# Row fetches split four and four behind the powers on GpSimd, in the last loop of a four-layer gated model

## The chip, the core and the metric

The kernel runs on one core of one Trainium2 chip. A core has five engines that run side by side, each through its own instructions in order: TensorE (PE, with its weight loads shown apart as PEld), VectorE (DVE), ScalarE (ACT), GpSimd (POOL) and SyncE (SP, which here only issues transfers). They wait for each other through semaphores. The metric is the device time of one execution, in microseconds, as the median of the runs.

## The reference

The input x has 32 sequences of 128 tokens with 128 features. Four layers follow each other, each an attention-like step and a feed-forward step whose results are added to x with a gate tanh(g). The last steps are the ones that matter here:

```python
x = x + jnp.tanh(g_ffn[2]) * _L2_ffn_ref(...)          # top 2 of 8 experts per token
x = x + jnp.tanh(g_xattn[3]) * _L3_xattn_ref(_layernorm(x), ctx_2048, ...)
x = x + jnp.tanh(g_ffn[3]) * _L3_ffn_ref(_layernorm(x), w_gate, w_up, w_down)
```

`_L2_ffn_ref` routes each token to two experts. `_L3_xattn_ref` (the depooling) takes a root-mean-square norm of its input, multiplies by a 128 x 128 matrix and a bias, and adds a decayed running sum of context patches. `_L3_ffn_ref` rounds its activations to integers by the largest value of each token, multiplies by ternary weights for gate and up, forms silu(gate) * up, rounds again in the same way and multiplies by the ternary down matrix.

## The kernel before, in words

The 32 sequences are handled as eight groups of four, so a group's x is a tile of 128 partitions (tokens) by 4 x 128 values. The x of all groups stays in SBUF for the whole kernel. The earlier layers and the mixture of experts run first. The experts leave their results in a table in DRAM, two rows for each token, and the running sums of the depooling lie in DRAM too. The last loop, which is all that the change touches, brings these together and runs the last feed-forward.

For each group g the loop has these parts:

- `fetch(g)` allocates the tiles `got` and `dp` (three buffers each), has SP load dp, and puts eight row fetches into the list `to_fetch`. A fetch is an indirect transfer issued by GpSimd (L821): it reads one row of the experts' table for each of 128 tokens. Eight of them fill `got`: four sequences by two experts. `move(to_fetch, n)` issues the first n of the list, or all.
- `depooled(g)` adds the fetched rows to x (eight instructions on VectorE, L833), takes the norm of x, transposes the result (TensorE, L272), scales it on ScalarE (hxT, L1344), multiplies it with `w_in` on top of dp (px, L1346 and L1348) and adds px to x (L280).
- `first(g)` takes the norm of x, quantizes it to integers (am, qt_x on VectorE, q_x on ScalarE), transposes it, forms the gate and up products (pg, pu, L1370 and L1372), silu on ScalarE (L1374) and the product h on VectorE (L1375).
- `second(g, h)` quantizes h (am, qt_h, q_h), transposes it, multiplies by the down matrix (po, L1391), scales it (L1396), adds it to x (L280) and has SP store x.

Both norms need a power of -0.5, and this power is computed on GpSimd. The statistics come from VectorE (L218 and L220). The norm of `depooled` computes two powers at once on eight columns (L254, tile w, operand made by L251 and L252). The norm of `first` computes one on four columns (L208, tile r, operand made by L207). VectorE then applies them (L241, tiles h and y). So the powers and the fetches share GpSimd, and GpSimd runs them in the order in which they stand.

The order within each engine is settled when the kernel is built: a scheduler sorts the instructions of an engine by what they depend on. The fetches are kept in program order. In the kernel before, `depooled(g)` calls `fetch(g + 1)` and `fetch(g + 2)` after its norm, and each `fetch` that has not been made yet issues its eight transfers at once. On GpSimd, eight fetches stand at the start, then the w of group 0, then sixteen fetches (groups 1 and 2), the w of group 1, eight fetches (group 3), the r of group 0, the w of group 2, eight fetches (group 4), the r of group 1, the w of group 3, and so on. The w of groups 6 and 7 have no fetches behind them.

Of the kernel before, what the change touches and what calls it, by code (L numbers as in the profile page):

```python
# [72 lines left out]
def tile_flamingo_gated(  # L73
# [22 lines left out]
    NG = B // NB  # L96
# [16 lines left out]
    xs = []  # L113
# [90 lines left out]
    def rsqrt(pool, v, eps=EPS):  # L204

        r = pool.tile([P, NB], F32, tag="r", name="r", bufs=4)
        nc.vector.tensor_scalar(r, v, eps, None, ALU.add)  # L207
        nc.gpsimd.tensor_tensor(r, r, m05.to_broadcast([P, NB]), ALU.pow)  # L208
        return r
# [30 lines left out]
                of = of.rearrange("p (h e d) -> p e h d", e=2, d=8)  # L240
            nc.vector.tensor_scalar(to, of, mv[:, b, 0:1], r[:, b : b + 1], ALU.subtract, ALU.mult)  # L241

    def layernorm(pool, a, tag="y", bufs=None, halves=False, again=None):

        mv = moments(pool, a)
        if again:

            w = pool.tile([P, 2, NB], F32, tag="w2", name="w2")  # L250
            nc.vector.tensor_scalar(w[:, 0], mv[:, :, 1], EPS, None, ALU.add)  # L251
            nc.vector.tensor_scalar(w[:, 1], mv[:, :, 1], 1.0 + EPS, EPS * EPS, ALU.mult, ALU.add)  # L252
            w2 = w.rearrange("p i b -> p (i b)")
            nc.gpsimd.tensor_tensor(w2, w2, m05.to_broadcast([P, 2 * NB]), ALU.pow)  # L254
            r, r2 = w[:, 0], w[:, 1]
        else:
            r = rsqrt(pool, mv[:, :, 1])
        y = None
        if tag:
            y = pool.tile([P, NB, D], F32, tag=tag, name="y", bufs=bufs)  # L260
            scaled(y, a, mv, r, halves)
        if not again:
            return y
        h = pool.tile([P, NB, D], F32, tag=again, name="h")
        scaled(h, a, mv, r2)
        return y, h
# [8 lines left out]
    def flat(a):  # L275
        return a.rearrange("p b s -> p (b s)")
# [114 lines left out]
    to_place, to_finish, to_fetch, to_store = [], [], [], []  # L391

    def move(queue, n=None):
        for do in queue[:n]:
            do()
        del queue[:n]
# [212 lines left out]
    class Routes:  # L609
# [205 lines left out]
        def fetch(self, pool, g, bufs=2):  # L815

            g -= self.begin
            got = pool.tile([P, 2, NB, D], F32, tag="got", name="got", bufs=bufs)

            def one(b, k):  # L820
                ins = nc.gpsimd.indirect_dma_start(  # L821
                    out=got[:, k, b, :], out_offset=None, in_=self.rows(),
                    in_offset=bass.IndirectOffsetOnAxis(ap=self.slot[:, g, k, b : b + 1], axis=0),
                )
                tc.keep_in_program_order(ins)

            to_fetch.extend(lambda b=b, k=k: one(b, k) for b in range(NB) for k in range(2))
            return got
# [77 lines left out]
    with ExitStack() as stack:  # L906
        w0 = load_weights(stack, W0, w0_d, W0.at, "w0")
        banks = attention_pools(stack, "s1", 1, 6)
        pool = banks[0]
# [210 lines left out]
    with ExitStack() as outer:  # L1120
# [3 lines left out]
        with ExitStack() as stack:  # L1124
            pool, psum = mlp_pools(stack, "f1")
# [24 lines left out]
        with ExitStack() as stack:  # L1150
            pool, psum_a, avs, _ = attention_pools(stack, "a2", 1, 4)
# [132 lines left out]
        with ExitStack() as stack:  # L1284
            pool, psum = mlp_pools(stack, "f2")
# [21 lines left out]
    with ExitStack() as stack:  # L1307
        stack.enter_context(nc.allow_low_precision(reason="small integers, exact in bfloat16"))
        pool, psum = mlp_pools(stack, "f3")
        wqd = wq["down"].rearrange("p (c o) -> p c o", c=4)  # L1310

        def quantized(a, n, tag):


            am = pool.tile([P, NB], F32, tag="am", name="am")
            nc.vector.tensor_reduce(am, a, AX.X, ALU.max, apply_absolute_value=True)
            inv = pool.tile([P, NB], F32, tag=f"inv_{tag}", name=f"inv_{tag}")
            nc.vector.tensor_scalar(inv, am, 1e-5, 1.0 / 127.0, ALU.max, ALU.mult)
            sc = pool.tile([P, NB], F32, tag="qs", name="qs")
            nc.vector.reciprocal(sc, inv)  # L1320
            t = pool.tile([P, NB, n], F32, tag=f"qt_{tag}", name=f"qt_{tag}")
            for b in range(NB):
                nc.vector.tensor_scalar(t[:, b, :], a[:, b, :], sc[:, b : b + 1], MAGIC, ALU.mult, ALU.add)
            q = pool.tile([P, NB, n], BF, tag=f"q_{tag}", name=f"q_{tag}")
            nc.scalar.add(q, t, -MAGIC)
            return q, inv

        fetched = {}

        def fetch(g):  # L1330
            if g < NG and g not in fetched:
                dp = pool.tile([P, NB, D], F32, tag="dp", name="dp", bufs=3)
                nc.sync.dma_start(out=flat(dp), in_=depool[g])
                fetched[g] = routes2.fetch(pool, g, 3), dp
                move(to_fetch)

        def depooled(g):
            got, dp = fetched[g]
            routes2.add(g, got)
            _, h = layernorm(pool, xs[g], tag=None, again="hx")  # L1340
            fetch(g + 1)
            fetch(g + 2)
            hT = pool.tile([P, NB, P], F32, tag="hxT", name="hxT")
            nc.scalar.mul(hT, transposed(psum, h), COL(col, "g_res"))  # L1344
            po = psum.tile([P, NB, D], F32, tag="y", name="px")
            nc.tensor.matmul(flat(po), lhsT=ident, rhs=flat(dp), start=True, stop=False, skip_group_check=True)  # L1346
            for b in range(NB):
                nc.tensor.matmul(  # L1348
                    po[:, b, :], lhsT=hT[:, b, :], rhs=W3(w3, "w_in"), start=False, stop=b == NB - 1,
                    skip_group_check=True,  # L1350
                )
            add_gated(xs[g], 3, po)

        def first(g):

            y = layernorm(pool, xs[g])
            q, inv = quantized(y, D, "x")
            tp = psum.tile([P, NB, P], BF, tag="tp", name="tpq")
            for b in range(NB):
                nc.tensor.transpose(tp[:, b, :], q[:, b, :], ident_b)  # L1360
            qT = pool.tile([P, NB, P], BF, tag="qT", name="qT")
            nc.scalar.copy(qT, tp)
            fg = pool.tile([P, 2, NB], F32, tag="fg", name="fg")
            nc.vector.tensor_tensor(
                fg, inv[:, None, :].to_broadcast([P, 2, NB]), winv[:, 0:2, None].to_broadcast([P, 2, NB]), ALU.mult
            )
            h = pool.tile([P, NB, 512], F32, tag="h", name="h")
            for b in range(NB):
                pg = psum.tile([P, 512], F32, tag="g", name="pg", bufs=4)
                nc.tensor.matmul(pg, lhsT=qT[:, b, :], rhs=wq["gate"], start=True, stop=True)  # L1370
                pu = psum.tile([P, 512], F32, tag="g", name="pu", bufs=4)
                nc.tensor.matmul(pu, lhsT=qT[:, b, :], rhs=wq["up"], start=True, stop=True)  # L1372
                sil = pool.tile([P, 512], F32, tag="sil", name="sil")
                nc.scalar.activation(sil, pg, AF.Silu, scale=fg[:, 0, b : b + 1])  # L1374
                nc.vector.scalar_tensor_tensor(  # L1375
                    h[:, b, :], pu, fg[:, 1, b : b + 1], sil, ALU.mult, ALU.mult
                )
            return h

        def second(g, h):  # L1380
            q, inv = quantized(h, 512, "h")
            hT = pool.tile([P, NB, 4, P], BF, tag="hT", name="hT")
            for b in range(NB):
                tp = psum.tile([P, 4, P], BF, tag="tp", name="tph")
                for c in range(4):
                    nc.tensor.transpose(tp[:, c, :], q[:, b, c * P : (c + 1) * P], ident_b)
                nc.scalar.copy(hT[:, b], tp)
            po = psum.tile([P, NB, D], F32, tag="y", name="po")
            for b in range(NB):
                for c in range(4):  # L1390
                    nc.tensor.matmul(  # L1391
                        po[:, b, :], lhsT=hT[:, b, c, :], rhs=wqd[:, c, :], start=c == 0, stop=c == 3
                    )
            nc.vector.tensor_scalar(inv, inv, winv[:, 2:3], None, ALU.mult)
            t = pool.tile([P, NB, D], F32, tag="scr", name="t")
            nc.vector.tensor_tensor(t, po, bc(inv), ALU.mult)  # L1396
            add_gated(xs[g], 7, t)
            nc.sync.dma_start(out=out[g * NB : (g + 1) * NB].rearrange("b s d -> s b d"), in_=xs[g])

        fetch(0)  # L1400
        depooled(0)
        depooled(1)
        h = first(0)
        for g in range(NG):
            if g + 2 < NG:
                depooled(g + 2)
            after = first(g + 1) if g + 1 < NG else None
            second(g, h)
            h = after
# [128 lines left out]
```

## Time and profile before

| what | value |
|---|---|
| median of three runs | 2208.09 us |
| lowest and highest of them | 2205.18 and 2213.33 us |
| the profiled execution's own time | 2221.3 us |
| its span, first to last instruction | 2219.6 us |
| mean granted TensorE clock | 0.853 |
| first fetch of the last loop | 2003.32 us from the start |
| w of groups 0 to 3 (L254, start) | 2016.04, 2037.91, 2052.09, 2081.12 us |
| w of groups 4 to 7 | 2104.55, 2128.72, 2152.24, 2171.38 us |
| fetches in the loop (L821 on POOL) | 64, median 0.949 us |
| powers in the loop | 8 of L254, mean 1.645 us; 8 of L208, mean 1.038 us |

The profile records one execution, whose own time stands above the runs' median. Its page cuts the span into forty slices and gives each engine's busy share of a slice in tenths. Its timeline lists each instruction with its start, its duration and, in brackets, how long the engine stood idle before it and what ended that. "issue" there is time in which the engine waited for nothing that the profile shows.

### The profile page before, as it was taken

Reading aid. Unit: us, or ns where it says so; the run is one execution under the profiler, and the core shown is the slowest. Engines: PE = TensorE matmul, PEld = TensorE weight load, DVE = VectorE, ACT = ScalarE, POOL = GpSimd, SP = SyncE. Lnnn points to the kernel's source line nnn. Section 1 sums busy time; section 2 is a strip of 40 time slices with the busy share of each in tenths; the row PEclk is TensorE's granted clock in tenths of the full one; section 3 lists DMA queues with packets and bytes.
Section 4 is the critical chain, followed back from the end, with each engine's and each line's share of the span. In section 5 each row is a group of like instructions: output and inputs, shape, how many; then the busy total and the mean of one; then the engine's idle time right before and its main releaser. Section 6 shows DMA issues by size and latency. Waiting matters only on the chain.

```text
span 2219.6 us, 35462 instructions
## 1 busy us (share of the span) xinstructions
PE 1666.0 (75%) x13618; PEld 1010.1 (46%) x13624; DVE 1205.2 (54%) x3480; ACT 894.5 (40%) x1110; POOL 648.9 (29%) x645
## 2 busy tenths in 40 slices
PE   0699998989999999888787399555756549992344
PEld 0454445456666666554455244244544424441222
DVE  7645455375545577676665333366556631113677
ACT  0376565556777655332333133211112114440334
POOL 5101011010100024355554570244544330006430
PEclk9999999999999999888877599867567669995676
DMA  6474558534333342222121154344333123332110
GB/s 213 146 243 166 179 200 270 170 104 121 99 94 88 110 114 72 59 53 58 51 60 34 59 158 147 110 114 137 111 101 115 43 85 123 132 112 71 30 37 19
DMA packets 164537, 244.66 MB, mean 110 GB/s; under 512 B 20561, under 2 KB 102289, under 8 KB 164113
## 3 DMA queue, kind: packets, MB, share of 16 engines
q1 hardware_dynamic: 156176, 225.62, 33.2%
q0 software_dynamic: 8192, 16.79, 2.6%
q8 instruction: 107, 1.75, 0.3%
q14 instruction: 62, 0.50, 0.1%
HBM read 139.74 MB, written 101.24 MB: 109 GB/s over the span
## 4 chain that ended last, share of the span: by engine, by line
PE 40%; DVE 14%; POOL 13%; issue 5%; DMA 3%; ACT 2%; another core or an unknown queue 2%; SPq 0%; POOLq 0%; DVEq 0%; ACTq 0%
PE ye L786 5%; PE av L581 4%; PE sct L498 4%; PE ph L1294 4%; PE ph L969 4%; POOL got L821 4%; PE sc L498 3%; POOL by_expert_r L636 3%; PE p L1135 2%; PE tpe L773 2%; PE p L1137 2%; POOL w L254 1%; PE tp L272 1%; DVE mx L529 1%
## 5 line engine op out<-in xcount | busy, mean ns | idle before, releaser
L564 ACT ACTIVATE w<-sct 128x1024 f32<-128x1024 f32 x288 | 292.9, 1025 | 355.2 <-PE sct L498 312.9
L529 DVE TENSOR_REDUCE mx<-sc 128x8 f32<-128x1024 f32 x160 | 194.9, 1219 | 138.5 <-PE sc L498 128.8
L498 PEld LDWEIGHTS <-stack_q 96*128 96x128 bf16 x2560 | 194.6, 109 | 130.7 <-issue 100.4
L581 PE MATMUL av<-w,va 128*9 128x128 f32 (+2 forms) x3584 | 207.6, 298 | 41.9 <-POOL w L567 26.5
L821 POOL DMA_INDIRECT got<-by_expert_r,slot_r x128 | 126.6, 989 | 336.8 <-issue 335.9
L534 DVE TENSOR_REDUCE mx<-sc 128x4 f32<-128x1024 f32 x128 | 152.9, 1221 | 132.8 <-PE sc L498 132.3
L498 PE MATMUL sc<-stack_k,stack_q 96*128 96x128 bf16 x1536 | 148.6, 245 | 47.1 <-DMA stack_k<-k 16.9
L498 PE MATMUL sct<-stack_q,stack_k 128*128 128x128 bf16 (+1 forms) x1536 | 145.3, 239 | 22.7 <-DVE mx L529 13.7
L498 PEld LDWEIGHTS <-stack_k 128*128 128x128 bf16 (+1 forms) x1536 | 114.1, 108 | 78.7 <-issue 75.3
L581 PEld LDWEIGHTS av<-w,va 128*9 128x9 f32 (+2 forms) x3584 | 101.1, 94 | 95.9 <-POOL w L567 38.1
L301 POOL CAST hml<-whole 128x512 bf16<-128x512 f32 (+1 forms) x56 | 37.3, 666 | 354.8 <-ACT whole L300 178.9
L786 PE MATMUL ye<-hid,w 128*128 128x512 f32 x276 | 133.4, 593 | 2.1 <-DVE hid L1140 2.1
L969 PE MATMUL ph<-h,w 128*128 128x512 f32 x256 | 123.7, 610 | 1.8 <-ACT hn L972 0.9
L208 POOL TENSOR_TENSOR r<-r,m 128x4 f32<-128x4 f32 x56 | 57.4, 1026 | 226.5 <-DVE r L207 175.1
L969 PE MATMUL ph<-hn,w 128*128 128x512 f32 x256 | 121.2, 604 | 0.7 <-ACT hn L972 0.7
L587 ACT COPY ot<-av 128x512 f32<-128x512 f32 x112 | 65.5, 584 | 110.6 <-PE av L581 97.5
L498 PE MATMUL sc<-stack_l,stack_q 96*128 96x128 bf16 x1024 | 109.7, 236 | 0.0
L567 POOL TENSOR_SCALAR_AFFINE_SELECT w<-w 128x1024 f32<-128x1024 f32 x64 | 71.1, 1112 | 113.1 <-ACT w L564 112.9
L498 PE MATMUL sct<-stack_q,stack_l 128*128 128x128 bf16 x1024 | 98.9, 234 | 4.9 <-DVE mx L529 4.9
L564 ACT ACT_TABLE_LOAD x72 | 92.4, 1283 | 9.7 <-PE sct L498 8.5
L593 PE MATMUL tpo<-cst,ot 128*128 128x128 f32 x448 | 79.3, 298 | 18.8 <-DVE mrows L550 9.9
L1294 PE MATMUL ph<-xT,w 128*128 128x512 f32 x184 | 86.6, 613 | 0.8 <-DVE nx L714 0.8
(288 smaller groups left out, 3260.6 us busy)
## 6 DMA issues: line engine op xcount, KB each, us to landing
by_expert_r<-zeros SPq DMA_DIRECT2D x40, 1024.0 KB
stack_q<-q SPq DMA_DIRECT2D x96, 288.0 KB
stack_k<-k SPq DMA_DIRECT2D x96, 288.0 KB
k<-hml SPq DMA_DIRECT2D x16, 1152.0 KB
w<-in_e_dram SPq DMA_DIRECT2D x23, 514.5 KB
xt<-by_expert_r SPq DMA_DIRECT2D x46, 256.0 KB
by_expert_r<-yt SPq DMA_DIRECT2D x46, 256.0 KB
q<-hml SPq DMA_DIRECT2D x72, 128.0 KB
```

The source lines that it names most:

```text
L498: nc.tensor.matmul(dst[:, h * P : (h + 1) * P], lhsT=stat[rows, 4 * e + h, b], rhs=mov[rows, 4 * e + h, b], start=start and h == e == 0, s ...
L529: nc.vector.tensor_reduce(mx[:, :, b0 : b0 + 2].rearrange("p h b -> p b h"), sc.rearrange("p i (h k) -> p i h k", h=4), AX.X, ALU.max, neg ...
L534: nc.vector.tensor_reduce(mx[:, :, b0], sc.rearrange("p i (h k) -> p h i k", h=4), AX.XY, ALU.max, negate=True,)
L564: nc.scalar.activation(w.rearrange("p i h k -> p i (h k)"), sc, AF.Exp)
L567: nc.gpsimd.affine_select(out=heads, in_=heads, pattern=[[0, 8], [1, P]], compare_op=ALU.is_ge, fill=0.0, base=0, channel_multiplier=-1,)
L581: nc.tensor.matmul(av[32 * h : 32 * h + dv + 1, b * P : (b + 1) * P], lhsT=values[c][:, b, 4 * u + h, :], rhs=w[:, i, h, :], start=c == 0, ...
L593: nc.tensor.transpose(tp[:, b].rearrange("p s r -> p (s r)"), ot[:, b, :], ident)
L636: ins = nc.gpsimd.indirect_dma_start(out=self.rows(), out_offset=bass.IndirectOffsetOnAxis(ap=slots, axis=0), in_=rows, in_offset=None,)
L786: nc.tensor.matmul(y, lhsT=w2[:, f, :], rhs=hid[:, f, :], start=f == 0, stop=f == n_f - 1)
L821: ins = nc.gpsimd.indirect_dma_start(out=got[:, k, b, :], out_offset=None, in_=self.rows(), in_offset=bass.IndirectOffsetOnAxis(ap=self.sl ...
L969: nc.tensor.matmul(ph, lhsT=wt[:, c, f * P : (f + 1) * P], rhs=h[:, c, :], start=c == 0, stop=c == 3)
L1294: nc.tensor.matmul(ph, lhsT=E2(w, "w1")[:, f * P : (f + 1) * P], rhs=xT, start=True, stop=True)
```

## The change

The fetches are no longer issued by `fetch`. The norm takes a function, `behind`, that it calls directly after the power has been issued. The norm of `depooled` issues four fetches there, the norm of `first` all that are left in the list. The main loop calls `fetch(g + 3)` just before `depooled(g + 2)`, so half of a group's rows stand behind the w of the group before it and half behind the r that follows. At the start, `first(0)` is moved in front of `depooled(1)`. All fetches of group 2 stand behind the w of group 1.

```diff
-    def layernorm(pool, a, tag="y", bufs=None, halves=False, again=None):
+    def layernorm(pool, a, tag="y", bufs=None, halves=False, again=None, behind=None):
...
             r = rsqrt(pool, mv[:, :, 1])
+        if behind:
+            behind()
         y = None
...
         def fetch(g):
-            if g < NG and g not in fetched:
+
+            if g < NG:
                 dp = pool.tile([P, NB, D], F32, tag="dp", name="dp", bufs=3)
                 nc.sync.dma_start(out=flat(dp), in_=depool[g])
                 fetched[g] = routes2.fetch(pool, g, 3), dp
-                move(to_fetch)
 
         def depooled(g):
-            got, dp = fetched[g]
+            got, dp = fetched.pop(g)
             routes2.add(g, got)
-            _, h = layernorm(pool, xs[g], tag=None, again="hx")
-            fetch(g + 1)
-            fetch(g + 2)
+            _, h = layernorm(pool, xs[g], tag=None, again="hx", behind=lambda: move(to_fetch, 4))
...
         def first(g):
 
-            y = layernorm(pool, xs[g])
+            y = layernorm(pool, xs[g], behind=lambda: move(to_fetch))
...
         fetch(0)
+        move(to_fetch)
+        fetch(1)
         depooled(0)
+        h = first(0)
+        fetch(2)
         depooled(1)
-        h = first(0)
+        move(to_fetch)
         for g in range(NG):
             if g + 2 < NG:
+                fetch(g + 3)
                 depooled(g + 2)
             after = first(g + 1) if g + 1 < NG else None
             second(g, h)
```

In the changed kernel the helpers of the fetch and of the addition have the lines L823 and L835, and that of the gated addition L282.

## The prediction

> **What bounds the kernel now.** I read the page's slices first, to see where the changed loop lies. It is the last four of the forty.
>
> ```profile
> span 2219.6 us, 35462 instructions
> ...
> PE   0699998989999999888787399555756549992344
> ...
> DVE  7645455375545577676665333366556631113677
> ...
> POOL 5101011010100024355554570244544330006430
> ```
>
> The last digits are 2344 for TensorE, 3677 for VectorE, 6430 for GpSimd: no engine is full, so a chain through several engines sets the time. Next I cut the loop at each eight-column power (L254, below w0 to w7 by group; r0 to r7 are the four-column powers of L208), with busy times per stretch: PE, PEld, DVE, ACT, POOL, granted clock, DMA share, GB/s.
>
> ```profile
> 2037.91:2052.09 14.18, 3.33 (x12) 2.50 (x12) 6.21 (x28) 0.69 (x1) 10.49 (x10) 0.50 0.15 42
> 2052.09:2081.12 29.03, 10.12 (x35) 4.36 (x36) 20.02 (x70) 10.99 (x15) 10.36 (x10) 0.56 0.07 18
> 2081.12:2104.55 23.43, 7.46 (x51) 6.17 (x53) 14.22 (x56) 5.54 (x9) 11.28 (x10) 0.65 0.16 46
> 2104.55:2128.72 24.17, 10.35 (x62) 6.08 (x62) 16.86 (x60) 9.54 (x14) 10.31 (x11) 0.71 0.16 43
> 2128.72:2152.24 23.52, 10.57 (x64) 6.39 (x64) 17.05 (x60) 8.78 (x14) 10.41 (x11) 0.65 0.13 35
> 2152.24:2171.38 19.14, 9.03 (x58) 5.38 (x57) 17.03 (x60) 7.91 (x13) 2.67 (x3) 0.68 0.04 14
> 2171.38:2219.60 48.22, 21.43 (x167) 14.25 (x166) 35.58 (x90) 23.82 (x36) 3.65 (x3) 0.71 0.07 22
> ```
>
> The line to see is the sixth. Between w6 and w7 VectorE does the same 60 instructions (17.03 us) as in the two steps before it, but POOL has 3 instructions where they have 11, and the step takes 19.1 us where they take 24.2 and 23.5. The eight missing instructions are the fetches. The timeline of POOL shows how they cost that (start, duration, idle before and its cause):
>
> ```profile
> 2104.55 1.64 POOL L254 TENSOR_TENSOR w<-w,m 128x8 f32<-128x8 f32 x1 [9.83 <-DVE w L252]
> 2106.36 1.02 POOL L821 DMA_INDIRECT got<-by_expert_r,slot_r  x1 [0.17 <-issue]
> ...
> 2115.18 0.94 POOL L821 DMA_INDIRECT got<-by_expert_r,slot_r  x1 [0.30 <-issue]
> 2116.15 1.04 POOL L208 TENSOR_TENSOR r<-r,m 128x4 f32<-128x4 f32 x1
> 2128.72 1.64 POOL L254 TENSOR_TENSOR w<-w,m 128x8 f32<-128x8 f32 x1 [11.53 <-DVE w L252]
> ...
> 2160.46 1.04 POOL L208 TENSOR_TENSOR r<-r,m 128x4 f32<-128x4 f32 x1 [6.59 <-DVE r L207]
> 2171.38 1.64 POOL L254 TENSOR_TENSOR w<-w,m 128x8 f32<-128x8 f32 x1 [9.87 <-DVE w L252]
> ```
>
> A fetch takes 0.95 us and 0.30 to the next: 1.25 each, eight in 10 us. The r behind them starts without any idle time, 11.6 us after its w, although its operand (L207, VectorE at 2109.35) was ready 6.8 us earlier. Then POOL stands idle for 11.5 us. What waits is VectorE, by its waits in the loop (total, times, longest):
>
> ```profile
> DVE y L241 <- POOL r L208: 22.8, 5, 7.8
> DVE x L833 <- DMA got<-by_expert_r,slot_r: 9.9, 11, 1.6
> DVE y L241 <- issue: 9.1, 2, 5.9
> DVE h L241 <- issue: 6.1, 1, 6.1
> ```
>
> The first and third are the r; the last is w1, which stands behind sixteen fetches.
>
> **The change part by part.** Nothing is computed more or less: 64 fetches, 8 w, 8 r, in another order. In the order of the built program everything before the loop is unchanged on all engines, and so is the order on SP's queue, so the eight loads of dp and the eight stores cost nothing new. POOL's order becomes: 8 fetches, w0, 4, r0, 4, w1, 8, w2, 4, r1, 4, w3, 4, r2, 4, and so on to 4, r5, 4, w7, r6, r7. VectorE's instructions are re-sorted too; I walk them with the trace's durations, starting at w0 = 2016.04, which stays.
>
> *Group 1.* Four fetches follow w0 and end at 2022.8. r0 now comes early: the addition of px (L280) ends at 2023.2 as before; four L218 (0.86), four L220 (0.36), an addition waiting for a landing at 2024.3 (0.35) and L207 (0.16) make it 2025.3. So r0 waits for VectorE, not for fetches, and ends at 2026.3; this is the price of the moved feed-forward, since the other four fetches of group 1 are queued behind it. They start at 2026.5 to 2030.2. From a fetch's start to the addition that consumes it the trace has 2.53 to 3.06 us (2017.90 to 2020.47; 2024.33 to 2027.39); with 2.6 the last lands at 2032.8. One addition, a statistics pair and L251/L252 (1.0 together): w1 at 2033.8, against 2037.91. VectorE's y, am and qt_x of group 0 (1.1, 0.6, 0.8) lie between those landings.
>
> *Group 2.* Eight fetches behind w1 (1.65): last start 2044.4, landed 2047.0; addition, four L218, four L220, w: 2.0. w2 at 2049.0, against 2052.09. The eight products of group 0 (L1375) fill the wait.
>
> *w2 to w3.* 1.65, then four fetches: r1 runs 2055.6 to 2056.6 (before: 2063.73). VectorE then does y 1.1, am 0.6, am of h 2.2, the addition of px 0.65, qt_x 0.8, qt_h 1.6, seven additions and small ones 2.7, statistics 1.4, two products 1.4: 12.5. w3 at 2069.1, against 2081.12: 12.0 us earlier. Of these, about 5 are the four fetches no longer before r1, 3.1 are w2's, and the rest is VectorE work of group 0 that now lies in the start's idle time.
>
> *The four steps w3 to w7.* From w to r: four fetches end at 1.65 + 0.17 + 4 x 1.25 - 0.3 = 6.5 us. In the undisturbed step r came 8.2 us after w6 because L207 stood behind the addition of px; in the new order it does so in the steps of w3 and w5, and before it in those of w4 and w6, as in the step of w7 (6.2 us). So r at 8.2 or, limited by fetches, 6.6. From r to the next w the undisturbed step took 10.9 (2160.46 to 2171.38) with the same instruction order. Steps of 19.1 and 17.5. I take 19.1 for two and, since VectorE's own work is 17.0 and leaves hardly a gap, 18.6 for two: 75.4, against 90.3. w7 at 2144.5, 26.9 earlier.
>
> *Landings.* The second four are now fetched in the step that uses them, a step ahead and no longer two. The last is consumed 9.25 us after r in the undisturbed step (2160.46 to 2169.71); it lands 1.05 + 0.17 + 3.75 + 2.6 = 7.6 us after r. Hidden, by 1.6 us; the next cover to go if fetches are slow.
>
> *Fetches beside a busy VectorE.* They ran mostly beside an idle one. Where one stood beside four L241 (2082.93) it took 1.01, and 1.90 once beside seven L833 (2085.50), against 0.95. A rule speaks against the change here. The Trainium skill, "SBUF — State Buffer", section "SBUF: two separate sides", says that while VectorE runs an operation that takes both ports GpSimd can't write a transfer's descriptors, and the transfer waits for its end. By the row 0.06 us a fetch: nothing. By the rule y (1.1) and qt_x (0.9) push the last fetch back by up to 2.0 us, 0.4 beyond the cover, in six steps 2.4 us. A bad case, the 1.90 for every second-half fetch, is 3.8 us a step, 2.2 beyond the cover, 13 us in all. A gain is excluded: 0.94 is the least. I take 0 and keep 13 for the range.
>
> *The rest.* After w7 there are no fetches before or after the change: 48.2 us either way. The granted clock (0.50 at the loop's start, 0.71 at its end) moves px between 274 and 582 ns a matmul; with denser work it may rise, or not: 2 us either way, 0 taken. One ACT hxT waited 5.3 us for something the trace calls "remote" at 2116; hidden now, it may come on the path or leave it, 5 us either way, 0 taken.
>
> Sum: 26.9 us off the profiled execution, 2219.6 of span and 1.7 around it: 2221.3 becomes 2194. That execution is 0.6% above the median of the runs, 2208.09; the same gain from there is 2181.
>
> **The rivals.**
>
> *Partial gain (chance 0.21).* Fetches slowed by VectorE, or a stall as above, eat 10 to 18 us: 2191 to 2199. For it: the 1.90 fetch and the thin 1.6 us. Against it: 1 of 64.
>
> *VectorE becomes the bound (0.08).* Steps at its 17.0 us of work, 68 for four, w7 at 2137: 34 us, 2174. Against it: gaps of some 2 us between dependent engines in the undisturbed step.
>
> *Landings become the bound, slower (0.05).* Place: the additions before each w. With a landing time L, w follows r after max(10.9, 6.6 + L). It bites from L = 4.3. To eat the 27 us and 11 more in six steps it must add 6.3 a step, L = 10.6 or more; at 11 the time is about 2222. Against it: all eleven waits for landings are at most 1.6 us, and no other load competes (DMA share 0.16 or less).
>
> *Nothing to measure (0.04).* The order is realised, but each step keeps 23.5 us for another reason: 2208. Against it: the 19.14 us step.
>
> **How the numbers follow.** The forecast has 0.62, with its own range of 21 to 33 us, 2175 to 2187. Half a percent, about what a measurement of this kernel can tell from no change, is 11 us; the three runs spread by 8. Faster by more: 0.62 + 0.08 + 0.18 of the partial gain, 0.88. Within: 0.07. Slower: 0.05. The range reaches to VectorE's bound with 3 us of spread, 2171, and into the partial gain, 2197.
>
> **What would show it.** Right: r without eight fetches before it, 6.5 to 8.5 us behind its w; w1 near 2034, w3 near 2069, steps of 17.5 to 19.5; VectorE's wait for L208 down from 32 us to below 10; no growing wait for got. Wrong: L823 rows clearly above 1 us, VectorE waiting for landings just before w, steps still above 22, or a first w1 later than 2038.

## The result, and the profile after

| what | before | after |
|---|---|---|
| median of four runs each, taken together | 2206.75 us | 2183.61 us |
| lowest and highest | 2205.18 and 2213.33 us | 2178.43 and 2190.39 us |
| ratio of after to before, 95% interval | | 0.9864, 0.9832 to 0.9895 |
| the profiled execution's own time, its span | 2221.3, 2219.6 us | 2190.4, 2188.7 us |
| mean granted TensorE clock | 0.853 | 0.855 |
| w0 to the end of the span | 203.56 us | 176.74 us |

The change made the kernel faster: by 23 us of 2207 by the two medians, whose quotient of 0.9895 is the upper end of the interval, and by 30 us by the ratio in the table. Why the two differ isn't on record. The two spans differ by 30.9 us, but 4.1 of them lie before the first w of the loop (2016.04 us before, 2011.96 after), where both programs are the same. In the profiled executions of this study w0 started anywhere between 1994 and 2018 us, so the clean measure of what happens in the loop is the time from w0 to the end. It fell by 26.8 us. Below it is called the loop time.

The page's slices, as they were read before (PE, DVE and POOL are the lines that answer to those shown there):

```profile
span 2188.7 us, 35469 instructions
...
PE   0699998989999999888887489826656629996354
...
DVE  7645445375645477677665333356656642113697
...
POOL 5101101020100013455554490063635340003550
```

VectorE's last four digits went from 3677 to 3697. The loop is still no stage of a single full engine, but in one slice of it VectorE is now above 90%. The cut at the eight-column powers shows the steps (length of the step; busy time and count of PE, PEld, DVE, ACT, POOL; granted clock, DMA share, GB/s):

```profile
2011.96:2029.79 17.83, 8.03 (x22) 3.79 (x22) 10.25 (x44) 3.83 (x6) 10.57 (x11) 0.50 0.16 45
2029.79:2045.04 15.25, 4.82 (x16) 3.23 (x16) 8.55 (x30) 2.65 (x5) 9.30 (x9) 0.50 0.14 35
2045.04:2065.27 20.23, 8.11 (x34) 4.79 (x35) 14.38 (x55) 6.09 (x9) 10.53 (x11) 0.50 0.10 26
2065.27:2084.02 18.75, 7.95 (x52) 4.78 (x51) 16.08 (x58) 6.29 (x10) 10.99 (x10) 0.68 0.20 58
2084.02:2102.60 18.58, 9.76 (x63) 5.96 (x62) 17.11 (x60) 8.44 (x14) 10.58 (x11) 0.68 0.20 56
2102.60:2121.10 18.50, 8.72 (x58) 4.93 (x57) 16.94 (x60) 7.91 (x13) 10.86 (x10) 0.68 0.17 44
2121.10:2139.78 18.68, 9.99 (x63) 6.12 (x61) 17.11 (x60) 8.43 (x14) 10.58 (x10) 0.68 0.16 42
2139.78:2188.70 48.92, 22.45 (x166) 14.24 (x163) 35.64 (x90) 23.65 (x35) 3.67 (x3) 0.71 0.07 22
```

The reader is to see that POOL still has its 10 or 11 instructions and 10.6 to 11.0 us of work in each of the four steady steps (w3 to w7), and that these steps take 18.6 us all the same, where the three with fetches took 23.4 to 24.2. VectorE's work in a full step is the same 17 us; it now fills 17 of 18.6. POOL's timeline in one steady step shows the new order (start, duration, idle before and its cause):

```profile
2102.60 1.66 POOL L254 TENSOR_TENSOR w<-w,m 128x8 f32<-128x8 f32 x1 [5.12 <-DVE w L252]
2104.45 1.08 POOL L823 DMA_INDIRECT got<-by_expert_r,slot_r  x1 [0.19 <-issue]
...
2108.34 1.23 POOL L823 DMA_INDIRECT got<-by_expert_r,slot_r  x1 [0.31 <-issue]
2110.12 1.07 POOL L208 TENSOR_TENSOR r<-r,m 128x4 f32<-128x4 f32 x1 [0.56 <-issue]
...
2115.28 0.94 POOL L823 DMA_INDIRECT got<-by_expert_r,slot_r  x1 [0.30 <-issue]
2121.10 1.67 POOL L254 TENSOR_TENSOR w<-w,m 128x8 f32<-128x8 f32 x1 [4.88 <-DVE w L252]
```

r starts 7.5 us after its w, against 11.6 us before. VectorE's waits in the loop (total, times, longest):

```profile
DVE x L835 <- DMA got<-by_expert_r,slot_r: 13.3, 13, 2.1
...
DVE y L241 <- POOL r L208: 7.8, 7, 4.3
DVE h L241 <- POOL w L254: 7.1, 8, 1.8
```

The wait for r fell from 31.9 us (22.8, and 9.1 of the kind that the trace calls issue) to 7.8. Of that, 4.3 is one wait in the step from w2, where r1 is still held by fetches. Its operand (L207) is ready at 2048.55, and r1 starts 3.2 us later, directly behind the last of the four:

```profile
2050.79 0.95 POOL L823 DMA_INDIRECT got<-by_expert_r,slot_r  x1 [0.30 <-issue]
2051.77 1.04 POOL L208 TENSOR_TENSOR r<-r,m 128x4 f32<-128x4 f32 x1
```

```profile
2048.38 0.17 DVE L207 TENSOR_SCALAR r<-bmv 128x4 f32<-128x4 f32 x1
2052.85 1.18 DVE L241 TENSOR_SCALAR y<-x,bmv,r 128x128 f32<-128x128 f32 x4 [4.30 <-POOL r L208]
```

The 6.1 us of h behind sixteen fetches are gone. The wait for got rose from 9.9 to 13.3 us; 12.1 of it lies before w2, in the start.

### The profile page after: what moved, and what is told of

Same layout as the page of the kernel before. It is cut to its first block, busy times and chain, and to the rows that moved or that the text cites. A ratio compares the mean times of both kernels' runs of the same rounds, so it can differ in the third digit from the quotient of the medians.

```text
span 2188.7 us, 35469 instructions
## 1 busy us (share of the span) xinstructions
PE 1671.2 (76%) x13624; PEld 1011.2 (46%) x13624; DVE 1204.9 (55%) x3480; ACT 893.6 (41%) x1110; POOL 648.0 (30%) x645
## 4 chain that ended last, share of the span: by engine, by line
PE 39%; DVE 14%; POOL 13%; issue 8%; DMA 2%; ACT 2%; another core or an unknown queue 1%; SPq 0%; POOLq 0%; DVEq 0%; ACTq 0%
PE ye L788 5%; PE av L583 4%; PE ph L1296 4%; PE sct L500 4%; POOL by_expert_r L638 4%; PE sc L500 3%; POOL got L823 3%; PE ph L971 3%; PE p L1137 2%; PE tpe L775 2%; PE p L1139 2%; POOL w L254 2%; DVE mx L531 1%; PE tp L274 1%; POOL r L208 1%
## 5 line engine op out<-in xcount | busy, mean ns | idle before, releaser
L583 PE MATMUL av<-w,va 128*9 128x128 f32 (+2 forms) x3584 | 207.0, 299 | 36.6 <-POOL w L569 23.9
L823 POOL DMA_INDIRECT got<-by_expert_r,slot_r x128 | 127.5, 996 | 336.5 <-issue 335.7
```

Of the source, the lines that this page charges most:

```text
L583: nc.tensor.matmul(av[32 * h : 32 * h + dv + 1, b * P : (b + 1) * P], lhsT=values[c][:, b, 4 * u + h, :], rhs=w[:, i, h, :], start=c == 0, ...
L823: ins = nc.gpsimd.indirect_dma_start(out=got[:, k, b, :], out_offset=None, in_=self.rows(), in_offset=bass.IndirectOffsetOnAxis(ap=self.sl ...
```

## The experiments

Each is compared with runs of the kernel before that were taken beside it. "Ratio" is to before, with its 95% interval; "loop" and "steps" are from one profiled execution each, and "tail" is the time from w7 to the end.

| run | ratio | w3 behind w0 | steps w3 to w7, us | tail | loop |
|---|---|---|---|---|---|
| before | 1 | 65.08 | 23.43, 24.17, 23.52, 19.14 | 48.22 | 203.56 |
| after | 0.9864 [0.9832, 0.9895] | 53.31 | 18.75, 18.58, 18.50, 18.68 | 48.92 | 176.74 |
| after, repeated | 0.9890 [0.9851, 0.9928] | 53.58 | 18.77, 18.67, 18.49, 18.67 | 48.67 | 176.85 |
| first(0) moved, alone | 0.9950 [0.9934, 0.9965] | 55.81 | 24.44, 22.58, 22.84, 19.31 | 48.31 | 193.29 |
| split, alone | 0.9888 [0.9840, 0.9937] | 56.49 | 18.63, 17.96, 19.41, 17.91 | 50.28 | 180.68 |
| eight behind w | 0.9959 [0.9943, 0.9976] | 54.56 | 23.85, 22.83, 22.59, 23.03 | 49.32 | 196.18 |
| eight behind r | 0.9942 [0.9919, 0.9965] | 53.28 | 21.87, 22.08, 22.20, 21.96 | 48.61 | 190.00 |
| two behind w, six behind r | 0.9916 [0.9885, 0.9947] | 53.20 | 19.51, 18.88, 21.24, 18.94 | 50.15 | 181.92 |
| group 1 whole behind w0 | 0.9903 [0.9871, 0.9936] | 52.75 | 18.74, 18.22, 19.49, 17.95 | 50.07 | 177.22 |
| half the maximum | 0.9793 [0.9754, 0.9831] | 52.55 | 17.55, 17.68, 17.62, 16.86 | 43.86 | 166.12 |
| half the fetches | 0.9819 [0.9768, 0.9870] | 45.87 | 18.10, 18.99, 18.76, 18.89 | 49.09 | 169.70 |
| y on ScalarE | 0.9908 [0.9875, 0.9941] | 51.23 | 20.84, 19.62, 19.24, 20.30 | 53.56 | 184.79 |
| a quarter of qt_h on ScalarE | 0.9858 [0.9834, 0.9882] | 51.55 | 19.21, 18.21, 19.09, 18.17 | 47.31 | 173.54 |
| that, and two fetches early | 0.9848 [0.9816, 0.9880] | 48.95 | 17.94, 17.80, 17.52, 18.55 | 48.19 | 168.95 |

The interval of a ratio reaches 3 to 11 us to either side. The loop time is finer, as the changed kernel run again shows: 176.74 and 176.85. That is one pair; how well the loop time of the other kernels repeats wasn't measured.

> The changed kernel once more, as a measure of how well the time from w0 to the end repeats. Both theories: 176 to 178.5 us from w0 to the end (176.7 in its first profile), whatever w0's own start is; a ratio to the kernel before near 0.986 to 0.99.

**The two parts, each alone.** First the kernel before with nothing but `first(0)` moved:

```diff
         depooled(0)
-        depooled(1)
         h = first(0)
+        depooled(1)
```

> The kernel before, with only first(0) moved in front of depooled(1); every fetch still issues its eight rows at once. My theory (what counts is how many fetches stand before a power that is ready): r0 now stands behind the sixteen fetches, w1 stays about 23 us after w0, the start gains some 6 us because the products of group 0 fall into idle time (w3 about 59 us after w0, before 65.1, changed kernel 53.3), and the steps w3 to w7 stay at 23.4, 24, 23.5 and 19.1 us. About 6 us faster than before, 2201. Rival (the moved feed-forward is what brings the gain): 15 us or more faster than before.

Then the changed kernel with `first(0)` back behind `depooled(1)`, and all of group 1's fetches behind w0:

```diff
         depooled(0)
-        h = first(0)
+        move(to_fetch)
         fetch(2)
         depooled(1)
         move(to_fetch)
+        h = first(0)
```

> The changed kernel with first(0) put back behind depooled(1), so the eight rows of group 1 stand in one piece behind w0; the halves stay from group 3 on. My theory: w1 about 15 us and w2 about 30 us after w0 (changed kernel 17.8 and 33.1), then a step w2 to w3 of some 24 us (changed 20.2) because the products of group 0 lie in it again; w3 about 54 us after w0, four steps of 18.6 us each. Within 2 us of the changed kernel, about 2185. Rival (the moved feed-forward is worth the 9 us that the step w2 to w3 lost): 2192 or more.

Measured: the moved feed-forward alone takes 10.3 us off the loop, the split alone 22.9, both together 26.8. The first is more than the 6 us that were expected. The second loop is 3.9 us longer than the changed kernel's, where at most 2 were expected: w2 came 33.4 us behind w0 and not 30. The two parts overlap by 6.4 us (10.3 + 22.9 - 26.8), and the table shows where: each alone brings w3 some 9 us closer to w0 (65.08 to 55.81 and to 56.49), both only 12 us. The steady steps are the split's alone: with the moved feed-forward the three with fetches stay at 22.6 to 24.4 us, with the split they are 18.5 us on average.

**Is it the four-and-four, or only that fetches are made a step later?** Two runs keep everything of the change but the split: all eight behind the w, or all behind the r.

```diff
-            _, h = layernorm(..., behind=lambda: move(to_fetch, 4))
+            _, h = layernorm(..., behind=lambda: move(to_fetch))
```

> The changed kernel with all eight rows behind w (of depooled) and none behind r, still one step ahead and with first(0) in front. My theory: r starts 11.6 us after w in each step, the step is 23.5 us, and so is the one from w6 to w7, which was free of fetches before; some 24 us slower than the changed kernel, about 2207, no better than before. Rival (fetching one step ahead or the moved feed-forward brings the gain, not the halves): at most 2190.

```diff
             if g + 2 < NG:
-                fetch(g + 3)
                 depooled(g + 2)
+                fetch(g + 3)
```

> The changed kernel with all eight rows of groups 3 to 7 behind r and none behind w. My theory: r is no longer held by fetches (6.2 to 8.2 us after w), but the last row lands 1.2 + 8.75 + 2.6 = 12.6 us after r and is needed 9.25 us after it, so w follows r after some 14.2 us: steps of 21 to 22 us (changed 18.6) with VectorE waiting for landings, some 10 us slower than the changed kernel, about 2194. Rival (landings are hidden in any order; only what stands before r counts): steps of 18.6 us or less, 2182 or less.

Eight behind w gives back 19.4 of the 26.8 us; some 24 were expected. Its steps are near those of before (22.6 to 23.9 us, now the fourth too), and POOL's timeline is that of before:

```profile
2098.76 1.63 POOL L254 TENSOR_TENSOR w<-w,m 128x8 f32<-128x8 f32 x1 [10.14 <-DVE w L252]
...
2109.45 0.95 POOL L823 DMA_INDIRECT got<-by_expert_r,slot_r  x1 [0.30 <-issue]
2110.43 1.04 POOL L208 TENSOR_TENSOR r<-r,m 128x4 f32<-128x4 f32 x1
2121.35 1.63 POOL L254 TENSOR_TENSOR w<-w,m 128x8 f32<-128x8 f32 x1 [9.88 <-DVE w L252]
```

r directly behind the last fetch, 11.7 us after w, and then 9.9 us in which POOL has nothing to do. Eight behind r gives back 13.3 us; some 10 were expected. Here r is early, 5.5 us behind w in the step shown next, but the last rows are late. VectorE's timeline at the end of that step:

```profile
2116.54 0.35 DVE L835 SCALAR_TENSOR_TENSOR x<-got,weight_r,x 128x128 f32<-128x128 f32 x1 [0.85 <-DMA got<-by_expert_r,slot_r]
...
2118.06 0.35 DVE L835 SCALAR_TENSOR_TENSOR x<-got,weight_r,x 128x128 f32<-128x128 f32 x1 [0.97 <-DMA got<-by_expert_r,slot_r]
...
2119.14 1.38 DVE L1375 SCALAR_TENSOR_TENSOR h<-pu,fg,sil 128x512 f32<-128x512 f32 x2
...
2121.34 0.16 DVE L251 TENSOR_SCALAR w<-bmv 128x4 f32<-128x4 f32 x1
```

Each of the last additions waits for a landing, one every 1.2 to 1.5 us, and three products of h then stand before L251. That is the rival "landings become the bound", seen at a smaller size. A split between the two,

```diff
-            ..., behind=lambda: move(to_fetch, 4))
+            ..., behind=lambda: move(to_fetch, 2))
```

> The changed kernel with two rows behind each w of depooled and six behind each r. My theory (1.6 us of cover over the last landing): the last row lands 1.2 + 6.25 + 2.6 = 10.1 us after r and is needed at 9.25, so VectorE waits some 0.8 us just before each w; steps w3 to w7 of 19.2 to 19.6 us (changed 18.6), 3 to 4 us more from w0 to the end, about 180. Rival (what stands before r is what counts): steps of 18.2 us or less, 175 us or less.

gave steps of 18.9 to 21.2 us and a loop 5.2 us longer than four and four: a little more than the 3 to 4 that were expected. r gained little from the two fetches that it no longer waits for: it came 7.1, 6.5, 9.0 and 6.5 us behind w, against 7.3 to 7.5 with four and four. VectorE's waits for landings came back, 3.9 us in six of them between w3 and w7. In the longest step, the one of 21.24 us, 1.60 us of waiting for TensorE's po lie before r as well, so not all of it is the landings' doing. In the step from w2 the smaller first part does help: r1 starts 4.2 us behind w2, and the step takes 17.74 us instead of 20.23.

**What bounds the steps now.** With the wait for r gone, VectorE's 17 us of 18.6 suggest VectorE. The next run halves its longest instruction.

```diff
-            nc.vector.tensor_reduce(am, a, AX.X, ALU.max, ...)
+            nc.vector.tensor_reduce(am, a[:, :, 0:256] if n == 512 else a, AX.X, ALU.max, ...)
```

The maximum over h then covers the first 256 of 512 columns; the other half is left out.

> The changed kernel with the maximum over h taken over the first 256 of its 512 columns (the scale of the second quantization is then that of half the values), which takes 1.1 us of VectorE's work out of each step and moves nothing else. Theory that VectorE's in-order work now sets the step: steps w3 to w7 of 17.5 us (changed 18.6), w2 to w3 19.1, the tail shorter by 1 to 3 us; from w0 to the end about 170 us. Rival (GpSimd's order or the landings set the step): steps unchanged at 18.5 or more, 174 us or more from w0 to the end.

The same cut at the powers, for the four steps of this kernel:

```profile
2066.53:2084.08 17.55, 6.71 (x42) 3.96 (x43) 14.89 (x58) 6.14 (x9) 10.99 (x10) 0.76 0.21 62
2084.08:2101.76 17.68, 8.91 (x62) 5.51 (x62) 16.17 (x60) 8.51 (x14) 10.57 (x11) 0.69 0.20 59
2101.76:2119.38 17.62, 8.27 (x57) 4.92 (x57) 16.05 (x60) 7.91 (x13) 10.98 (x10) 0.69 0.16 46
2119.38:2136.24 16.86, 8.55 (x62) 5.40 (x61) 15.96 (x60) 8.33 (x14) 10.47 (x11) 0.70 0.17 47
```

VectorE has 0.9 to 1.2 us less work in a step, and the steps are 0.9 to 1.8 us shorter (the 1.8 in the last of them, where TensorE's clock also rises 2.7 us earlier; the run with two fetches early, below, shows what that does). The tail lost 5 us, more than the 1 to 3 expected. So the instruction is on the path. It does not follow that any VectorE work is: the maximum stands between r and the next w, on the chain itself.

Two runs that move VectorE work to ScalarE ask about that. The first moves y, 1.25 us for four on VectorE:

```diff
-            nc.vector.tensor_scalar(out[:, b, :], a[:, b, :], ...)            # y, L241
+            nc.scalar.activation(out[:, b, :], a[:, b, :], AF.Identity, bias=nb[:, b : b + 1], scale=r[:, b : b + 1])
```

> The changed kernel, with y of first's layer norm (L241's four tensor_scalars on VectorE, 0.4 us each by their rows) made on ScalarE instead: four Identity activations with scale r and bias -mean*r, and one small VectorE instruction for the bias. Theory: VectorE, busy 17.0 of every 18.6 us step, bounds the loop since the wait for r is gone (the run with half the maximum took 1.0 us off each step); y's 1.3 to 1.6 us a step leave it, so the steps w3 to w7 fall to 17.3-17.8 and the loop from w0 to the end to 170-174 us. Rival: y now waits for r in ScalarE's order, and what stands behind it there (qt_h's readers and the silu pieces) comes later, so VectorE waits for am as it waited for r: steps of 18.6-19.5 and a loop of 177-184 us, with a VectorE wait on ScalarE that isn't in the changed kernel. I hold the rival as likely as the theory.

The rival won, with 8.0 us more in the loop: 184.8 us, just above the 177 to 184 that it had. But the wait for ScalarE that it named isn't there; from w3 to w7 VectorE waits for w (5.9 us), landings (2.9) and r (1.9). One step of it, then VectorE's timeline there:

```profile
2096.10:2115.34 19.24, 11.02 (x60) 6.35 (x61) 15.93 (x56) 9.97 (x17) 10.93 (x10) 0.68 0.16 42
```

```profile
2097.80 0.60 DVE L250 TENSOR_SCALAR h<-x,bmv,w 128x128 f32<-128x128 f32 x2 [1.46 <-POOL w L263]
...
2103.80 0.35 DVE L844 SCALAR_TENSOR_TENSOR x<-got,weight_r,x 128x128 f32<-128x128 f32 x1 [1.37 <-DMA got<-by_expert_r,slot_r]
...
2107.05 0.67 DVE L1327 TENSOR_REDUCE am<-y 128x4 f32<-128x512 f32 x1
```

Against the changed kernel's step at 2084.02 VectorE has 1.2 us less work, and 3.3 us idle instead of 1.5. The maximum of y starts 10.95 us after w; in the changed kernel (at 2093.76) it is 9.74, with y's own 1.25 us inside. VectorE's instructions were sorted into another order, and idle waits for w and for a landing took the place of y. In this step TensorE's clock rises 7.0 us behind w, against 2.8 in the one that it is compared with, so a part of the delay may be TensorE's. The tail is 4.6 us longer too.

The second moves one of the four instructions of qt_h, and stays out of the way of r:

```diff
+                if n == 512 and b == 3:
+                    nc.scalar.activation(t[:, b, :], a[:, b, :], AF.Identity, bias=magic, scale=sc[:, b : b + 1])
+                else:
                     nc.vector.tensor_scalar(t[:, b, :], a[:, b, :], sc[:, b : b + 1], MAGIC, ALU.mult, ALU.add)
```

> The changed kernel, with one of the four 512-column instructions of the first rounding step (L1325, VectorE, about 0.4 us) made on ScalarE (Identity, scale and a bias tile), about 0.7 us there. Theory: VectorE bounds each step, so each falls by 0.3-0.4 us to 18.2-18.4 and the loop from w0 to the end to 173-175 us. Rival: q_h, the matmul's left side, is later by the 0.3 us by which ScalarE is slower, and ScalarE's in-order queue is as full as VectorE's where it matters: steps as in the changed kernel or longer by up to 0.5 us, a loop of 177-181 us.

The loop came out where the theory put it, 173.54, but not for its reason. The four steps sum to 74.68 us, against 74.51 in the changed kernel: nothing. What fell is w2 to w3 (by 1.7 us) and the tail (by 1.6). In the steps the 0.4 us that VectorE gained came back as waits for TensorE, in front of t; its waits from w3 to w7, the changed kernel first:

```profile
DVE t L1396 <- PE tp L274: 1.0, 2, 0.8
DVE t L1396 <- PE po L1391: 0.7, 1, 0.7
```

```profile
DVE t L1401 <- PE tp L274: 3.3, 3, 1.3
DVE t L1401 <- PE px L1353: 1.3, 1, 1.3
```

1.7 us became 4.6. So here VectorE waited for what TensorE hands to t, ahead of r in VectorE's order. Whether that must follow from the edit is another question: the last run below has the same work in these steps, and there the wait for t is 1.2 us.

**What do the fetches still cost?** Here each group has four fetches instead of eight, two behind each power. Left out are the rows of each token's second expert; the first expert's rows are added again in their place.

```diff
-            to_fetch.extend(lambda b=b, k=k: one(b, k) for b in range(NB) for k in range(2))
+            to_fetch.extend(lambda b=b, k=k: one(b, k) for b in range(NB) for k in range(1 if bufs == 3 else 2))
...
-            ..., behind=lambda: move(to_fetch, 4))
+            ..., behind=lambda: move(to_fetch, 2))
```

> The changed kernel with four fetches for each group instead of eight, two behind each power; left out are the rows of each token's second expert, in whose place the first expert's rows are added again, so that VectorE has the same instructions. It asks what the 32 fetches that fall away still cost in the changed kernel. Theory: in the steps w3 to w7 fetches are hidden, both before r (which waits for VectorE's L207) and before the next w, so the four steps stay at 18.3 to 18.8; only the start, where VectorE waits for landings, gets shorter (13.3 us of waits for got in the loop, of which some 2.5 us at group 1 and 5 us at group 2 go), so that w3 comes 5 to 9 us earlier behind w0 and the loop takes 168 to 172 us. Rival: four fetches before r and four behind it still bind the steps, in turns with VectorE; then each of the four steps falls by 1 us or more, to 17.5 or less, and the loop to 166 us or less.

The theory held. The four steps:

```profile
2048.37:2066.47 18.10, 7.96 (x52) 4.89 (x51) 15.79 (x58) 6.30 (x10) 6.90 (x6) 0.69 0.15 45
2066.47:2085.46 18.99, 10.30 (x63) 6.16 (x61) 17.10 (x60) 8.45 (x14) 6.78 (x7) 0.68 0.15 42
2085.46:2104.22 18.76, 9.01 (x58) 5.11 (x57) 16.98 (x60) 7.91 (x13) 6.79 (x6) 0.68 0.11 29
2104.22:2123.11 18.89, 10.20 (x63) 6.13 (x61) 17.09 (x60) 8.45 (x14) 6.78 (x7) 0.68 0.10 28
```

POOL has four instructions and 4 us less in each, and the sum is 74.74 us against 74.51. TensorE's clock rises 0.6 us later here on average, which may hide something: by the table of the last run below, an estimate of one to three microseconds in the four steps. But the changed kernel's own timeline points the same way: in three of its four steps r starts directly behind L207 and not behind a fetch, and one wait for a landing is left, 1.2 us. So in the steady steps the fetches cost little any more. In the start they still cost 7.4 us, by which w3 is closer to w0 here; 2.5 of them lie in the step from w2, where r1 comes 4.2 us behind w2 instead of 6.7.

**What the start still holds.** With group 1's eight fetches in one piece behind w0, r0 behind them:

```diff
         depooled(0)
+        move(to_fetch)
         h = first(0)
```

> The changed kernel with all eight rows of group 1 behind w0, so r0 stands behind them, and first(0) still in front. My theory: the last row of group 1 lands 13.2 us after w0 and w1 follows at 15.1 (changed 17.8); w2 30.2 after w0 (changed 33.1); later steps as in the changed kernel. 2 to 3 us faster from w0 to the end, about 174. Rival (the later r0 pushes the products of group 0 into the step w2 to w3): no gain, 176 to 179 us.

This missed: w1 stayed at 17.76 us behind w0. The rows landed earlier, but nothing could use them, by VectorE's timeline:

```profile
2027.35 0.39 DVE L835 SCALAR_TENSOR_TENSOR x<-got,weight_r,x 128x128 f32<-128x128 f32 x1 [0.65 <-DMA got<-by_expert_r,slot_r]
2030.73 1.11 DVE L241 TENSOR_SCALAR y<-x,bmv,r 128x128 f32<-128x128 f32 x4 [3.00 <-POOL r L208]
2031.76 0.34 DVE L835 SCALAR_TENSOR_TENSOR x<-got,weight_r,x 128x128 f32<-128x128 f32 x1
```

The last three additions of group 1 stand behind y of group 0, and y waits 3.00 us for r0, which now starts behind the eight fetches. What a changed POOL order is worth depends on VectorE's order, and in that order the three additions stayed behind y.

The last run fills POOL's idle time ahead of w0 with two of group 1's fetches, on top of the quarter of qt_h; `first(0, 4)` issues four fetches behind r0:

```diff
         fetch(1)
+        move(to_fetch, 2)
         depooled(0)
-        h = first(0)
         fetch(2)
+        h = first(0, 4)
         depooled(1)
```

> Two edits on top of the changed kernel: the quarter of qt_h on ScalarE as in the run before last, and two of group 1's fetches made ahead of w0, where POOL stands idle for 2.95 us, so that behind r0 two fetches of group 1 and two of group 2 stand, and six instead of eight of group 2 behind w1. Theory: at the start each fetch less before a power is worth 1.25 us (half the fetches brought w3 7.4 us closer to w0), so w2 comes 2.5 us earlier behind w1 (12.7 instead of 15.2 us), w0 itself at most 1.2 us later, since an addition of group 1 now stands before its operand on VectorE, and the loop takes 170 to 172 us against 173.5. Rival: in VectorE's order two additions of group 2 stand before w1's operand, and they wait for the same four fetches behind r0, so what w2 gains is given back in the next step, where VectorE is the bound: a loop of 173 to 175 us.

w2 came 12.71 us behind w1, as the theory said, and the loop took 168.95 us, better than both theories. w0 paid for it: 13.3 us from the first fetch to w0, against 12.7 without the early fetches. From the first fetch to the end this kernel takes 182.3 us, the changed kernel 189.6. Over the quarter alone, 186.3, the start accounts for 2.0 us (w2 2.6 closer to w0, w0 0.6 later). The steady steps are 2.9 us shorter, 71.8 against 74.7, with the same work, and the tail is 0.9 longer. Nothing of the theory explains the 2.9 us. What differs is the moment at which TensorE speeds up. The two matmuls of dp into px in one such step, by PE's timeline, here and without the early fetches:

```profile
2063.09 1.02 PE L1351 MATMUL px<-dp,cst 128*128 128x512 f32 x2
```

```profile
2110.02 1.49 PE L1351 MATMUL px<-dp,cst 128*128 128x512 f32 x2
```

The mean granted clock of the two steps is nearly the same, 0.69 and 0.68. In short windows (the clock is the third number from the end) it changes within the step:

```profile
2062.00:2063.00 1.00, 1.00 (x11) 0.72 (x10) 0.85 (x3) 1.00 (x3) 0.81 (x2) 0.84 0.00 0
2063.00:2069.00 6.00, 3.79 (x32) 2.53 (x30) 5.02 (x16) 2.42 (x5) 4.89 (x5) 1.00 0.42 121
```

```profile
2110.00:2111.00 1.00, 1.00 (x3) 0.46 (x2) 0.67 (x2) 0.35 (x1) 0.73 (x1) 0.53 0.20 61
2111.00:2117.00 6.00, 3.18 (x30) 2.19 (x28) 4.00 (x16) 1.27 (x2) 3.76 (x5) 1.00 0.27 80
```

With two fetches early the clock rises from 0.50 to 1.00 at 2062.3, 1.5 us behind this step's w; without them at 2110.9, 3.9 us behind it. Both kernels have the same instructions from w3 to w7, in the same order on GpSimd and ScalarE and nearly so on VectorE, and over their eight steps the later rise mostly goes with the longer step:

| clock rises, us behind w | 0.8 | 1.5 | 1.7 | 1.9 | 2.4 | 3.7 | 3.8 | 3.9 |
|---|---|---|---|---|---|---|---|---|
| step, us | 17.52 | 17.80 | 18.21 | 18.17 | 17.94 | 18.55 | 19.21 | 19.09 |

The quarter alone has the 1.7, 1.9, 3.8 and 3.9, this kernel the other four. In the step from w6 VectorE's order is the same too, and there this kernel is the slower one, 18.55 us against 18.17, with the rise at 3.7 against 1.9. So the 2.9 us go with the clock and are no gain shown for the early fetches, and that the quarter alone left the steps as they were is no proof that it must. What sets the moment wasn't tried. It isn't chance from run to run: in the changed kernel the clock rises 1.0, 2.8, 1.3 and 3.3 us behind w3 to w6, in its repetition 0.8, 2.5, 1.0 and 3.0. This last kernel is the shortest in the loop of all that compute the whole result. By the median of the runs, 0.9848 [0.9816, 0.9880], it can't be told from the changed kernel, whose gain of 7 us would be 0.3%.

## Why the prediction was right, point by point

| step, us behind w0 | forecast | measured |
|---|---|---|
| w1 | 17.8 | 17.83 |
| w2 | 33.0 | 33.08 |
| w3 | 53.1 | 53.31 |
| four steps w3 to w7 | 75.4 | 74.51 |
| tail | 48.2 | 48.92 |
| loop, less than before | 26.9 | 26.82 |

*What bounded the kernel before* was read rightly: r behind eight fetches. That r comes early once only half of the fetches stand before it, and that the next w then follows some 11 us later, is what the timelines show. Putting the eight back behind w brings back the 11.7 us from w to r and steps of 23.

*The start.* The walk with the trace's durations came within 0.3 us at each of three powers, r1 with its 6.7 us behind w2, limited by fetches (6.6 forecast), included. Its parts were measured apart only roughly: the moved feed-forward alone gave 10.3 us where about 6 were expected of it, probably because without the split it also takes group 0's work out of the step to w3, which fell from 29.0 to 21.4 us.

*The four steps.* The sum was 0.9 us off, and the inside was wrong. The forecast had r at 8.2 us in two steps and at 6.6, set by the fetches, in the two others, hence steps of 19.1 and 18.6. Measured, r comes 7.3 to 7.5 us behind w in all four, and the next w 11.0 to 11.5 behind r, where 10.9 were forecast. The term that failed is "limited by fetches, 6.6" for the steps of w4 and w6: r came no sooner than 7.4 us there, and with only two fetches in front 7.2 to 7.8. L207 on VectorE sets it in three of the four steps: in the one at 2084.02 it ended at 2091.31, and r started at 2091.40. In the first of them L207 and the last fetch ended together, at 2072.46. L207 stood behind the addition of px in the steps of w3 and w5 and ahead of it in the two others, as forecast; what the forecast lacked is that it also stands behind t, and so behind TensorE and the moment at which its clock rises. That the sum came out so well is in part luck, since an r too late in two steps and too early in two cancel. The pair of the forecast does exist: with the split alone the clock rises 0.7, 3.2 and 0.9 us behind w4, w5 and w6, r comes 6.7, 8.4 and 6.7 us behind them, and the steps are 17.96, 19.41 and 17.91 us.

*Landings.* They are hidden in the steady steps, as forecast; half the fetches make the four steps no shorter. One sign that the forecast named didn't hold: the wait for got did grow, from 9.9 to 13.3 us, of which 12.1 lie ahead of w2. That the cover is thin was right too. Two more fetches behind r bring the waits back, and eight cost 13 us. From w3 to w7 the changed kernel has one such wait, 1.2 us.

*Fetches beside a busy VectorE.* The trace and the rule of the Trainium skill ("SBUF — State Buffer", section "SBUF: two separate sides") stood against each other here, and the row decided for the changed kernel. All 64 fetches of the loop, many of them beside VectorE's densest work (min, median, max in ns):

```profile
L823 POOL DMA_INDIRECT got<-by_expert_r,slot_r x64: 940/957/1335, 1999.1 to 2133.7; - x64
```

The median is 0.957 us, against 0.949 before. In all 13 profiles with 64 fetches the medians are 0.949 to 0.960; the longest single fetch is the 1.90 us of before, and 1.40 in the changed orders. The 0.06 us that the forecast put down to VectorE is no clear sign of it: the loop's very first fetch, at 2003.32 before, takes 0.99 us with VectorE idle. Some slowing is seen all the same. With eight behind r, one fetch in each of the four steps starts beside the four instructions of qt_h, and it takes 1.19 to 1.23 us. That fits the rule in its direction, at 0.3 us and not at the 2.0 that the forecast had by it. In the changed kernel no fetch stands there; its two longest, 1.33 and 1.23 us, start beside the additions of L282, and why they are long is open. The bad case of 13 us fell.

*The rest.* The mean granted clock was the same (0.855 and 0.853). Its moment within the step, which the forecast left out, moves single steps by about a microsecond. The tail took 0.7 us more where nothing was forecast.

*The rivals.* VectorE as the bound is half true. The steps stopped at 18.6 us, not at its 17.0, because waits for TensorE, r and w remain; with y moved to ScalarE such waits took the place of the work. The slower rival, the landings, needs 10.6 us from a fetch's start to its use; nothing like it was seen. The run with all eight behind r shows its mechanism, at up to 1.1 us a landing.

## What to carry to other kernels

When compute and transfer issues share an in-order engine, the place to look is the step in which the issues are missing: here one undisturbed step of the old profile gave the size of the gain to 1 us a step. Split the issues so that each part fits in the time in which that engine would be idle, in front of each result that others wait for, and count the landing time of the last part against its use; both one-sided splits lose. Once the gap is closed, check for the next bound before moving work between engines: one that is 92% busy need not be the bound, and an instruction taken off it may only turn into a wait. And before a difference of a microsecond in a step is put down to an edit, compare the clock within the step: here its mean was the same where its moment was not.

## What the hardware showed that was not expected

- An indirect fetch of 128 rows takes GpSimd 0.95 us in the median before the change, and 0.96 after it with more of VectorE's work beside it; beside qt_h it took 1.2.
- ScalarE took 0.80 us for the 128x512 instruction of qt_h that VectorE did in 0.48 us (0.42 from one to the next), and 0.48 us for each 128x128 piece of y.
- TensorE's granted clock switches between 0.50 and 1.00 within each steady step. In the changed kernel, read in windows of 0.1 us, it stayed at 1.00 for 6.8 to 6.9 us and at 0.50 for 10.2 to 10.3 or 13.6 to 13.7 us; all of these are close to multiples of 3.4 us. The same two matmuls took 1.02 and 1.49 us in steps whose mean clock was 0.69 and 0.68.
- Where the loop begins varied by some 20 us between runs: in those with the same instructions ahead of it w0 started at 1997.5 to 2018.1 us. A gain of 0.3% is seen in the loop's own time, not in the kernel's median.
